# A graph-attention layer with residual and norm: x of row blocks 22 and 23 moved behind the adjacency, added by GpSimd and normalised by VectorE

## The chip, the cores and the metric

The kernel runs on one core of a Trainium2 chip. The metric is the device time of one execution in microseconds. The kernel before takes 233.9 us, the median of 3 runs (233.88 to 234.27).

## The reference

x is 4096 x 512, adj is 4096 x 4096, W is 512 x 2048 (four heads of 512 columns), a holds two vectors of 512 for each head; all are fp32. What is computed:

```python
ht = (x @ W).reshape(N, 4, 512).transpose(1, 0, 2)
e = leaky_relu(src[:, :, None] + dst[:, None, :], 0.01) + adj[None]
att = softmax(e, axis=-1)
out = layernorm(x + einsum('hij,hjd->hid', att, ht).mean(axis=0))
```

`src` and `dst` are the products of `ht` with the halves of `a`. The entries of adj are zero or go up to 1e9, so that in nearly every row the softmax is one at the largest entry of adj and zero elsewhere.

## The kernel before

**What a row needs.** The kernel finds, for each row of adj, the column of its largest entry, gathers that row of x (`y`), multiplies it with the mean of the four heads of W (`w_sum`), adds the row's own x and normalises. A test at the end (`bound`, `test`, `count`, `report`) compares the lead of the largest entry over the second with a bound from the norms of x, W and a; where it fails, a general path (`general`) computes the block in full. With these inputs the general path does not run.

**Blocks.** The 4096 rows are 32 blocks of 128 (`ib` 0 to 31). The names used below: `P` = 128, `NB` = 32, `Q` = 4, `LATE` = 28, `BEHIND` = 24. One block of adj is 2 MB in a tile `adj_t` of a pool with six buffers; one block of x is 256 KB in a row of `hold`, which also holds the results until they are stored.

**The loop.** Step `t` runs over 0 to 31. In step t the sync queue (SP) issues the load of adj block t + 5, ahead of it in some steps a load of x (`x_at`, `load_x`). VectorE takes the segment maxima of adj block t (L212), finds the segment of the largest entry (`find_segment`), and, one or two steps later, the column inside the segment (`find_column`). GpSimd computes the addresses and starts the two gathers for a block: the segment of adj (`lead`, L230) and the row of x (`y`, L250 and L255). TensorE and ScalarE work on block t - 3: `spread` and `from_table` for rows whose partner lies in block 0, `turn` (the transposes at L284 and the copy `yt` at L286), `residual` (x added by a product with the identity, L296) and `products` with `w_sum` (L303). Statistics and normalising (`row_norm`, `parked_stats`, `root`, `scales`, `finish`) follow on ScalarE and GpSimd some steps later.

**The blocks from 24 on.** Blocks 24 to 27 have no residual product. Their sums are copied from PSUM by `put_by` into a spare tile of the adj pool; x of 24 to 27 is loaded into `hold` behind adj 31, and GpSimd adds it in the drain (`add_x`, L357). From block 25 on the last product of a block is put off behind the next block's transposes. Blocks 28 to 31 are normalised by VectorE (`moments`, `factor`, `normalise`).

**The drain.** Behind the loop an order written out by hand follows: the last row norms, the stores of finished blocks, the last two columns (block 31 by an index over the whole row, L278), the last turns and products, the test, and the statistics of 24 to 31 between them. `bound(0)` is a reduction of `xx`, the row norms, on VectorE (`xm`, L498) and a small transpose on TensorE (`px`, L500); `bound(2)` is a product (L505), and `bound(3)` writes `lead_by` on ScalarE (L507). The program order is the order of execution on each engine: nothing is reordered by a scheduler.

Of the kernel before, what the change touches and what calls it, by code (L numbers as in the profile page):

```python
# [9 lines left out]
F32 = mybir.dt.float32  # L10
# [3 lines left out]
AF = mybir.ActivationFunctionType  # L14
# [7 lines left out]
P = 128  # L22
# [51 lines left out]
def leading_rows(ctx, tc, x, adj, W, a, out, ident, leads, any_bad):  # L74
# [8 lines left out]
    nc = tc.nc  # L83
    N, D = x.shape
    H = a.shape[0]
    KB, NB = D // P, N // P
    RB = NB - 1
    AHEAD = 5
    Q = 4
    PIECES = 4  # L90
    LATE = NB - Q
    BEHIND = LATE - Q

    landing = ctx.enter_context(tc.tile_pool(name="landing", bufs=1))
    landing.tile([P, 24], F32, name="pad")
    hold = landing.tile([P, NB, D], F32, name="hold")
    a_rows = landing.tile([2 * H, D], F32, name="a_rows")
    adj_pool = ctx.enter_context(tc.tile_pool(name="adj_pool", bufs=AHEAD + 1))
# [11 lines left out]
    x_rows = x[P:, :].rearrange("(p nb) d -> p nb d", nb=RB)  # L110
# [4 lines left out]
    w_at = NB - KB * H  # L115
    w_sum = once.tile([P, KB, D], F32, name="w_sum")
    adj_t = {}

    def pieces(ib):
        return PIECES if ib == NB - 1 else 2 if ib >= LATE else 1  # L120
# [9 lines left out]
    def load_x(lo, n):  # L130
        if lo == 0:
            nc.sync.dma_start(hold[:, 0, :], x[:P, :])
            lo, n = 1, n - 1
        if n:
            nc.sync.dma_start(hold[:, ds(lo, n), :], x_rows[:, ds(lo - 1, n), :])

    def load_w(kb, n):
        nc.sync.dma_start(hold[:, ds(w_at + kb * H, n * H), :], w_blocks[:, ds(kb * H, n * H), :])
# [17 lines left out]
    for e, lo, hi in spans:  # L156
        if lo == 0:
            nc.gpsimd.iota(first[:, 0:1], pattern=[[0, 1]], base=0, channel_multiplier=N // e)
            lo = 1
# [28 lines left out]
    xx = once.tile([P, NB], F32, name="xx")  # L188
# [9 lines left out]
    seg_of, at_of, lead_of, y_t, yt_of, o_ps = {}, {}, {}, {}, {}, {}  # L198
# [64 lines left out]
    def find_inner(ib):  # L263
        nc.vector.max(out=inner[:, ib, :], in_=lead_of[ib])  # L264

    def find_column(ib):
        if ib < BEHIND:
            find_inner(ib)
# [20 lines left out]
    def turn(ib):  # L289
        yt_of[ib] = turned_rows(y_t.pop(ib))  # L290
# [7 lines left out]
    def products(ib, lo=0, hi=KB):  # L298
        start = ib not in o_ps
        if start:  # L300
            o_ps[ib] = psum.tile([P, D], F32, name="o")
        for kb in range(lo, hi):
            nc.tensor.matmul(  # L303
                o_ps[ib], yt_of[ib][:, kb, :], w_sum[:, kb, :],
                start=(start and kb == 0), stop=(kb == KB - 1),
            )
# [37 lines left out]

    def row_norm(ib):
        sq = rows.tile([P, D], F32, name="sq")
        nc.scalar.activation(sq, hold[:, ib, :], AF.Square, accum_out=xx[:, ib : ib + 1])  # L347

    def put_by(ib):

        if ib == BEHIND:
            o_ps["by"] = adj_pool.tile([P, N // D, D], F32, name="adj_t")
        nc.scalar.copy(o_ps["by"][:, ib - BEHIND, :], o_ps.pop(ib))

    def add_x(ib):
        o = o_ps[ib] = o_ps["by"][:, ib - BEHIND, :]
        nc.gpsimd.tensor_add(o, o, hold[:, ib, :])  # L357

    def add_sums(ib, out):
        nc.vector.tensor_add(out, o_ps[ib], hold[:, ib, :])  # L360
# [2 lines left out]
    def stats(ib):  # L363
        o, i = o_ps[ib], slice(ib, ib + 1)
        sq = rows.tile([P, D], F32, name="sq")
        nc.scalar.activation(sq, o, AF.Identity, scale=-1.0 / D, accum_out=nm[:, i])
        sq = rows.tile([P, D], F32, name="sq")
        nc.scalar.activation(sq, o, AF.Square, bias=nm[:, i], accum_out=sd[:, i])  # L368
# [10 lines left out]
    def scales(i):  # L379
        nc.gpsimd.tensor_mul(nm[:, i], nm[:, i], sd[:, i])  # L380
        nc.gpsimd.tensor_scalar(sd[:, i], sd[:, i], -float(D), None, op0=OP.mult)
# [6 lines left out]
    def finish(ib):  # L388
        i = slice(ib, ib + 1)
        o = hold[:, ib, :] if ib < BEHIND else o_ps.pop(ib)  # L390
        nc.scalar.activation(hold[:, ib, :], o, AF.Identity, bias=nm[:, i], scale=sd[:, i])  # L391
# [15 lines left out]
    def moments(ib):  # L407

        if ib < NB - 1:
            st = small.tile([P, nc.vector.BN_STATS_DIM], F32, name="st", bufs=2)  # L410
            nc.vector.bn_stats(st, o_ps[ib])
        else:
            st = halves_st
        mv = mean_var[ib] = small.tile([P, nc.vector.BN_AGGR_DIM], F32, name="mv", bufs=3)
        nc.vector.bn_aggr(mv, st)
        r = rt[ib] = sd[:, ib : ib + 1]
        nc.scalar.activation(r, mv[:, 1:2], AF.Sqrt, bias=eps)

    def factor(ib, shift=False):
        nc.vector.reciprocal(rt[ib], rt[ib])  # L420
        if shift:
            nc.vector.scalar_tensor_tensor(
                nm[:, ib : ib + 1], mean_var[ib][:, 0:1], -1.0, rt[ib], op0=OP.mult, op1=OP.mult
            )

    def normalise(ib, o, columns=slice(0, D)):
        nc.vector.tensor_scalar(
            hold[:, ib, columns], o, mean_var[ib][:, 0:1], rt[ib], op0=OP.subtract, op1=OP.mult
        )
# [12 lines left out]
    def store(queue, lo, n):  # L442
        if lo == 0:
            queue.dma_start(out[:P, :], hold[:, 0, :])
            lo, n = 1, n - 1
        queue.dma_start(out_rows[:, ds(lo - 1, n), :], hold[:, ds(lo, n), :])
# [82 lines left out]
    def report(pg):  # L529
        nc.vector.tensor_scalar(any_bad, pg, -1.0, float(N), op0=OP.mult, op1=OP.add)  # L530

    x_at = {lo - 1 - lo // (5 * Q): (lo, Q) for lo in range(Q, BEHIND, Q)}
    squares = list(range(KB * H))
    squares_at = {t: 2 if t < 7 else 1 for t in range(3, 15)}
    COLUMN, PROJECT, STATS = 2, 3, 4
    FACTORS = (*((lo, lo + Q) for lo in range(0, BEHIND - Q, Q)), (BEHIND - 4, BEHIND - 2), (BEHIND - 2, BEHIND))
    FINISHED = {t: (t - 11,) for t in range(11, 28)}
    FINISHED |= {28: (17, 18), 29: (19, 20)}

    def lag_of(hi):  # L540
        return hi - 1 + STATS + (3 if hi < BEHIND - 2 else 2)

    WHOLE = range(12, 20)
    END = (*range(1, 3), *range(5, 20))
# [1 line left out]
    for t in range(NB):  # L546
        if t == NB // 2:
            tc.mark_branch_hint_location("general", engines=HINTED)
        if t in x_at:
            load_x(*x_at[t])  # L550
        if t + AHEAD == NB - 1:
            load_x(LATE, 2)
        load_adj(t + AHEAD)
        middle = PIECES if t in END else 1 if t == NB - 1 else 2
        segment_maxima(t, 0, middle)
        if t >= COLUMN and t not in END and t != COLUMN + 1:
            find_column(t - COLUMN)
            if t == lag_of(BEHIND) + 1:
                scales(slice(BEHIND - 2, BEHIND))
        if t not in END:  # L560
            segment_maxima(t, middle, PIECES)
        if t == NB - 1:
            for ib in (BEHIND, LATE + 2, BEHIND + 2):
                load_x(ib, 2)
        find_segment(t)
        if t in END:
            find_column(t - 1 if t <= COLUMN else t - COLUMN)
        if t + 1 in TABLED:
            clear_rows(t + 1)
        for lo, hi in FACTORS:  # L570
            if t == lag_of(hi):
                nc.vector.reciprocal(sd[:, lo:hi], sd[:, lo:hi])
                if hi < BEHIND:
                    scales(slice(lo, hi))
        if t < 2:
            mean_of_heads(t)
        elif t == 2:
            mean_of_heads(2)
            mean_of_heads(3)
            fill_table()  # L580
        if t == 0:
            square_sums_of_a()
        if 21 <= t < 24:
            head_norms(t - 21)
        ib = t - PROJECT
        if t == NB - 2:
            finish(BEHIND - 3)
            finish(BEHIND - 2)
        if t == NB - 1:
            row_norm(LATE)  # L590
            row_norm(LATE + 1)
            finish(BEHIND - 1)
            residual(LATE + 1)
        if ib >= 0:
            if ib in TABLED:
                spread(ib)
            turn(ib)
            if ib > BEHIND:
                products(ib - 1, KB - 1, KB)
            if ib < BEHIND:  # L600
                residual(ib)
            if ib in TABLED:
                from_table(ib)
            products(ib, 0, KB if ib < BEHIND else KB - 1)
            if ib == 0:
                split_table()
        for _ in range(squares_at.get(t, 0)):
            square_sum_of_w(squares.pop(0))
        if t >= BEHIND + STATS:
            put_by(t - STATS)  # L610
        elif t >= STATS:
            row_norm(t - STATS)
            parked_stats(t - STATS)
        for lo, hi in FACTORS:
            if t == hi - 1 + STATS:
                root(slice(lo, hi))
        for done in FINISHED.get(t, ()):
            finish(done)

    for ib in (BEHIND, LATE + 2):  # L620
        row_norm(ib)
        row_norm(ib + 1)
    for ib in range(0, BEHIND - Q, 2):
        store(nc.sync, ib, 2)
    store(nc.sync, BEHIND - Q, Q)
    find_column(NB - 2)
    add_x(BEHIND)
    add_x(BEHIND + 1)
# [4 lines left out]
    turn(NB - 3)  # L633
    row_norm(BEHIND + 2)
    row_norm(BEHIND + 3)
    nc.scalar.activation(xx, xx, AF.Sqrt, scale=1.05 ** 2)
    residual_in_halves(NB - 1)
    products(NB - 3, 0, 2)
    stats(BEHIND)
    bound(0)  # L640
    add_sums(LATE, o_ps[LATE])
# [230 lines left out]
```

## Time and profile before

| what | value |
|---|---|
| median of 3 runs | 233.9 us (233.88 to 234.27) |
| the profiled execution's own time | 233.53 us |
| its span, first to last instruction | 232.0 us |
| bytes moved by DMA | 96.04 MB at a mean of 414 GB/s |
| mean granted TensorE clock | 0.98 |

The page of the profile gives the busy time of each engine as a share of the span, then the span in 40 slices of 5.8 us with the busy share of each slice in tenths. The chain of work that ended last is followed back from the last instruction: at each step to what released it, or to the instruction before it on its engine. A row of the timeline gives start, length, engine, line and operation, the tile written and those read, the shapes and the count; in brackets stand the engine's idle time before it and what ended that. PE is TensorE, DVE VectorE, ACT ScalarE, POOL GpSimd and SP the sync engine. A line such as L357 can be that of a helper, so blocks are told apart by time. A DMA's landing is counted from its issue.

### The profile page before, as it was taken

How to read it: one execution, taken by the hardware profiler on the slowest of the kernel's cores; microseconds unless marked ns; L12 is line 12 of the kernel's file. 1: busy time of each engine (PE TensorE's matmuls, PEld its weight loads, DVE VectorE, ACT ScalarE, POOL GpSimd, SP SyncE). 2: the span in 40 equal slices, each digit the busy share in tenths (PEclk: the TensorE clock that was granted, in tenths of full speed). 3: DMA queues.
4: the chain of work that ended last, by engine and by line, in shares of the span. 5: the costliest groups of instructions: out<-in, count | busy, mean ns of one | idle time of the engine just before them, and what ended most of it. 6: DMA issues, size and time to landing. Idle time of an engine off the chain costs nothing.

```text
span 232.0 us, 2532 instructions
## 1 busy us (share of the span) xinstructions
PE 197.6 (85%) x604; PEld 95.5 (41%) x614; DVE 189.6 (82%) x296; ACT 153.2 (66%) x378; POOL 111.5 (48%) x254
## 2 busy tenths in 40 slices
PE   0069988779099999997999899999999999999990
PEld 0033443334044444443444345454544444545460
DVE  0448289899879997999699959996999999967882
ACT  3003213588075987797998678878888877958872
POOL 4020414525554556355635665554565665637620
PEclk9999999999859999999999999999999999999997
DMA  6999999999999999999999999999999999999995
GB/s 221 426 435 428 433 421 437 425 431 411 440 429 422 420 437 427 429 421 434 418 433 430 417 435 429 419 430 431 426 432 415 419 425 416 419 416 419 420 374 207
DMA packets 13379, 96.04 MB, mean 414 GB/s; under 512 B 2148, under 2 KB 2596, under 8 KB 7984
## 3 DMA queue, kind: packets, MB, share of 16 engines
q1 hardware_dynamic: 9792, 88.08, 90.0%
q0 software_dynamic: 3552, 7.73, 8.5%
q8 instruction: 6, 0.10, 0.2%
q14 instruction: 13, 0.11, 0.1%
q10 hardware_dynamic: 16, 0.02, 0.0%
HBM read 88.51 MB, written 8.39 MB: 418 GB/s over the span
## 4 chain that ended last, share of the span: by engine, by line
DMA 44%; PE 30%; DVE 19%; ACT 2%; issue 1%; POOL 1%; DVEq 0%; POOLq 0%; ACTq 0%
DMA adj_t<-in_adj_dram 39%; PE o L303 19%; DVE seg L212 15%; DMA y<-in_x_dram,col 4%; PE o L296 3%; PE o L343 3%; PE tp L284 3%; PE o L400 2%; DVE at L224 1%; DVE top L222 1%; DMA a_rows<-in_L_gnn_a_dram 1%; DVE inner L264 1%; POOL lead L230 0%; PE o L396 0%; ACT sq L368 0%
## 5 line engine op out<-in xcount | busy, mean ns | idle before, releaser
L212 DVE TENSOR_REDUCE seg<-adj_t 128x128 f32<-128x2048 f32 (+4 forms) x54 | 138.9, 2589 | 27.4 <-DMA adj_t<-in_adj_dram 27.4
L303 PE MATMUL o<-w_sum,yt 128*128 128x512 f32 x248 | 113.5, 598 | 1.1 <-ACT yt L286 0.8
L303 PEld LDWEIGHTS o<-w_sum,yt 128*128 128x128 f32 x248 | 46.8, 192 | 49.0 <-issue 42.0
L230 POOL DMA_INDIRECT lead<-in_adj_dram,row x31 | 32.5, 1050 | 14.5 <-POOL row L226 14.5
L255 POOL DMA_INDIRECT y<-in_x_dram,col x27 | 29.1, 1077 | 12.1 <-POOL col L272 6.1
L226 POOL TENSOR_TENSOR row<-at,first 128x1 uint32<-128x1 uint32 x31 | 5.8, 188 | 60.0 <-DVE at L224 43.6
L284 PE MATMUL tp<-ident,y 128*128 128x128 f32 x128 | 22.9, 302 | 12.0 <-DMA y<-in_x_dram,col 11.9
L286 ACT COPY yt<-tp 128x512 f32<-128x512 f32 x33 | 19.0, 576 | 14.2 <-PE tp L284 13.9
L451 PE MATMUL o<-hold,ident 128*128 128x512 f32 x32 | 16.4, 671 | 14.0 <-DMA hold<-in_L_gnn_W_dram 14.0
L284 PEld LDWEIGHTS tp<-ident,y 128*128 128x128 f32 x128 | 18.3, 210 | 23.9 <-issue 17.8
L296 PE MATMUL o<-hold,ident 128*128 128x512 f32 x50 | 26.5, 612 | 0.0
L333 ACT ACTIVATE off<-px,minus 128x128 f32<-128x128 f32 x27 | 9.9, 366 | 19.9 <-PE px L331 19.8
L343 PE MATMUL o<-z,pick 128*128 128x512 bf16 x72 | 20.4, 386 | 1.1 <-ACT pick L335 0.8
L347 ACT ACTIVATE sq<-hold 128x512 f32<-128x512 f32 x32 | 20.0, 625 | 0.0
L391 ACT ACTIVATE hold<-hold,nm,sd 128x512 f32<-128x512 f32 x24 | 18.8, 801 | 0.0
L374 ACT ACTIVATE sq<-hold,nm 128x512 f32<-128x512 f32 x24 | 17.3, 722 | 0.8
L452 ACT ACTIVATE w_sum<-o 128x512 f32<-128x512 f32 x4 | 2.4, 597 | 22.5 <-PE o L451 22.5
L245 ACT COPY y<-zero 128x512 f32<-128x512 f32 x27 | 16.3, 603 | 0.0
L451 PEld LDWEIGHTS o<-hold,ident 128*128 128x128 f32 x32 | 6.7, 216 | 22.9 <-issue 21.6
L343 PEld LDWEIGHTS <-pick 128*128 128x128 bf16 x81 | 7.8, 100 | 19.9 <-issue 10.5
L372 ACT ACTIVATE hold<-o 128x512 f32<-128x512 f32 x24 | 14.3, 597 | 0.8
L222 DVE MAX8 top<-seg 128x8 f32<-128x256 f32 (+2 forms) x31 | 11.3, 366 | 1.1
(117 smaller groups left out, 190.3 us busy)
## 6 DMA issues: line engine op xcount, KB each, us to landing
adj_t<-in_adj_dram SPq DMA_DIRECT2D x28, 2048.0 KB, 33.1
adj_t<-in_adj_dram SPq DMA_DIRECT2D x6, 1024.0 KB, 27.3
out_dram<-hold SPq DMA_DIRECT2D x12, 512.0 KB, 10.1
hold<-in_x_dram SPq DMA_DIRECT2D x5, 1024.0 KB, 33.0
hold<-in_L_gnn_W_dram SPq DMA_DIRECT2D x2, 2048.0 KB, 16.5
hold<-in_x_dram SPq DMA_DIRECT2D x4, 512.0 KB, 12.7
adj_t<-in_adj_dram SPq DMA_DIRECT2D x4, 512.0 KB, 18.6
out_dram<-hold SPq DMA_DIRECT2D x4, 256.0 KB, 2.8
```

What stands on the lines that cost most here:

```text
L212: nc.vector.tensor_reduce(seg_of[ib][:, ts(k, N // e // n)], adj_t[ib][:, ts(k, N // n)].rearrange("p (s e) -> p s e", e=e), axis=AX.X, op ...
L230: nc.gpsimd.indirect_dma_start(out=lead, out_offset=None, in_=adj_segs[e], in_offset=bass.IndirectOffsetOnAxis(ap=row[:, :1], axis=0),)
L255: nc.gpsimd.indirect_dma_start(out=y_t[ib], out_offset=None, in_=x, in_offset=bass.IndirectOffsetOnAxis(ap=col[:, :1], axis=0), bounds_che ...
L284: nc.tensor.transpose(tp[:, kb, :], y[:, ds(kb, P, KB)], ident)
L286: nc.scalar.copy(yt, tp)
L296: nc.tensor.matmul(o_ps[ib], ident, hold[:, ib, :], start=start, stop=False)
L303: nc.tensor.matmul(o_ps[ib], yt_of[ib][:, kb, :], w_sum[:, kb, :], start=(start and kb == 0), stop=(kb == KB - 1),)
L343: nc.tensor.matmul(o_ps[ib], pick, z[k], start=(start and k == 0), stop=False)
L347: nc.scalar.activation(sq, hold[:, ib, :], AF.Square, accum_out=xx[:, ib : ib + 1])
L374: nc.scalar.activation(sq, hold[:, ib, :], AF.Square, bias=nm[:, i], scale=-float(D), accum_out=sd[:, i])
L391: nc.scalar.activation(hold[:, ib, :], o, AF.Identity, bias=nm[:, i], scale=sd[:, i])
L451: nc.tensor.matmul(o, ident, hold[:, w_at + kb * H + h, :], start=(h == 0), stop=(h == H - 1))
```

## The change

`PUT` = 22 is new. Blocks 22 and 23 join the path of blocks 24 to 27, with these differences: x of 22 to 27 is loaded behind adj 31 into a spare tile of the adj pool (`late_x`), the sums of 22 to 27 are copied from PSUM into `hold`, and GpSimd adds there in place. Blocks 22 and 23 lose their residual product, their parked statistics on ScalarE, their root, factors and finish; instead VectorE takes their moments and normalises them in the drain, ahead of `bound(0)`. x of 20 and 21 is loaded alone in step 19, where x of 20 to 23 was loaded in step 18. The row norms of 28 and 29 move from step 31 to step 30. The row norms of 22 and 23 move into the drain, ahead of those of 24, 25, 30 and 31. The stores of blocks 0 to 7 go out in fours, and the store of 20 to 23 is split in two.

```diff
+    PUT = BEHIND - 2
...
+    late_x = []
...
-            nc.sync.dma_start(hold[:, ds(lo, n), :], x_rows[:, ds(lo - 1, n), :])
+            to = late_x[0][:, ds(lo - PUT, n), :] if PUT <= lo < LATE else hold[:, ds(lo, n), :]
+            nc.sync.dma_start(to, x_rows[:, ds(lo - 1, n), :])
...
     def row_norm(ib):
         sq = rows.tile([P, D], F32, name="sq")
-        nc.scalar.activation(sq, hold[:, ib, :], AF.Square, accum_out=xx[:, ib : ib + 1])
+        x_of = late_x[0][:, ib - PUT, :] if PUT <= ib < LATE else hold[:, ib, :]
+        nc.scalar.activation(sq, x_of, AF.Square, accum_out=xx[:, ib : ib + 1])
 
     def put_by(ib):
-
-        if ib == BEHIND:
-            o_ps["by"] = adj_pool.tile([P, N // D, D], F32, name="adj_t")
-        nc.scalar.copy(o_ps["by"][:, ib - BEHIND, :], o_ps.pop(ib))
+        nc.scalar.copy(hold[:, ib, :], o_ps[ib])
+        o_ps[ib] = hold[:, ib, :]
 
     def add_x(ib):
-        o = o_ps[ib] = o_ps["by"][:, ib - BEHIND, :]
-        nc.gpsimd.tensor_add(o, o, hold[:, ib, :])
+        nc.gpsimd.tensor_add(o_ps[ib], o_ps[ib], late_x[0][:, ib - PUT, :])
...
-    x_at = {lo - 1 - lo // (5 * Q): (lo, Q) for lo in range(Q, BEHIND, Q)}
+    x_at = {lo - 1: (lo, Q) for lo in range(Q, BEHIND - Q, Q)}
+    x_at[PUT - 3] = (BEHIND - Q, 2)
...
-    FACTORS = (*((lo, lo + Q) for lo in range(0, BEHIND - Q, Q)), (BEHIND - 4, BEHIND - 2), (BEHIND - 2, BEHIND))
+    FACTORS = (*((lo, lo + Q) for lo in range(0, BEHIND - Q, Q)), (BEHIND - Q, PUT))
...
-            if t == lag_of(BEHIND) + 1:
-                scales(slice(BEHIND - 2, BEHIND))
...
         if t == NB - 1:
-            for ib in (BEHIND, LATE + 2, BEHIND + 2):
+            late_x.append(adj_pool.tile([P, N // D, D], F32, name="adj_t"))
+            for ib in (PUT, BEHIND, LATE + 2, BEHIND + 2):
                 load_x(ib, 2)
...
         if t == NB - 2:
             finish(BEHIND - 3)
-            finish(BEHIND - 2)
-        if t == NB - 1:
             row_norm(LATE)
             row_norm(LATE + 1)
-            finish(BEHIND - 1)
+        if t == NB - 1:
             residual(LATE + 1)
...
-            if ib < BEHIND:
+            if ib < PUT:
                 residual(ib)
...
-        if t >= BEHIND + STATS:
+        if t >= PUT + STATS:
             put_by(t - STATS)
...
-    for ib in (BEHIND, LATE + 2):
+    for ib in (PUT, BEHIND, LATE + 2):
         row_norm(ib)
         row_norm(ib + 1)
-    for ib in range(0, BEHIND - Q, 2):
+    for ib in range(0, 2 * Q, Q):
+        store(nc.sync, ib, Q)
+    for ib in range(2 * Q, PUT, 2):
         store(nc.sync, ib, 2)
-    store(nc.sync, BEHIND - Q, Q)
+    add_x(PUT)
+    add_x(PUT + 1)
     find_column(NB - 2)
     add_x(BEHIND)
     add_x(BEHIND + 1)
...
     row_norm(BEHIND + 2)
     row_norm(BEHIND + 3)
+    moments(PUT)
+    moments(PUT + 1)
     nc.scalar.activation(xx, xx, AF.Sqrt, scale=1.05 ** 2)
     residual_in_halves(NB - 1)
     products(NB - 3, 0, 2)
+    for ib in (PUT, PUT + 1):
+        factor(ib)
+        normalise(ib, o_ps.pop(ib))
+    store(nc.sync, PUT, 2)
     stats(BEHIND)
     bound(0)
     add_sums(LATE, o_ps[LATE])
```

More of the change, by code (lines that the diff above doesn't have):

```diff
@@ L540, in lag_of @@
     def lag_of(hi):
-        return hi - 1 + STATS + (3 if hi < BEHIND - 2 else 2)
+        return hi - 1 + STATS + (3 if hi < PUT else 2)
     WHOLE = range(12, 20)
@@ L572, in leading_rows @@
                 nc.vector.reciprocal(sd[:, lo:hi], sd[:, lo:hi])
-                if hi < BEHIND:
-                    scales(slice(lo, hi))
+                scales(slice(lo, hi))
         if t < 2:
```

## The prediction

> **What bounds the kernel now.** I read the page's engine and DMA rows first, then the chain of work that ended last, then the timelines of the four engines from block 22 on.
>
> ```profile
> PE 197.6 (85%) x604; PEld 95.5 (41%) x614; DVE 189.6 (82%) x296; ACT 153.2 (66%) x378; POOL 111.5 (48%) x254
> DMA  6999999999999999999999999999999999999995
> DMA packets 13379, 96.04 MB, mean 414 GB/s; under 512 B 2148, under 2 KB 2596, under 8 KB 7984
> ```
>
> Three resources are near full at once. The DMA engines are full in every slice but the first and the last, and the change moves no byte more or less: it can only reorder them. So the question is which work waits for which in the last 30 us.
>
> ```profile
> 215.42 0.11 PE px L500
> 215.53 0.86 PE o L303 x2
> 216.39 0.32 PE px L505 x2
> ...
> 216.74 0.35 ACT lead_by L507
> ...
> 221.68 0.70 ACT hold L391
> 222.38 0.48 ACT yt L286
> ```
>
> The chain passes through one narrow place in the drain: the small transpose px at L500 (`bound(0)`), which needs VectorE's `xm`, then px at L505, then ScalarE's `lead_by`. Behind it the chain follows ScalarE's square roots and statistics to `yt` of block 31 and its products, with hand-overs of some hundredths: whatever delays px at L500 delays the end.
>
> **The change part by part.**
>
> *The x loads.* Before, 1 MB of x (blocks 20 to 23) stands in the queue ahead of adj 23. Now half of it stands ahead of adj 24, and x of 22 and 23 follows adj 31.
>
> ```profile
> 158.53 2.29 DVE L212 TENSOR_REDUCE seg<-adj_t 128x64 f32<-128x2048 f32 x1 [2.00 <-DMA adj_t<-in_adj_dram]
> 164.16 2.28 DVE L212 TENSOR_REDUCE seg<-adj_t 128x64 f32<-128x2048 f32 x1
> L128 SPq DMA_DIRECT2D adj_t<-in_adj_dram x1: 327/327/327, 130.2 to 130.2; - x1
> DMA to landing us min/median/max: 33.8/33.8/33.8
> ...
> 208.46 0.09 DVE L270 MATCH_VALUE_LOAD within<-top,lead 128x8 f32 x1 [1.83 <-DMA lead<-in_adj_dram,row]
> 208.77 4.42 DVE L278 FIND_INDEX8 col<-top,adj_t 128x8 uint32<-128x4096 f32 x1
> 214.91 0.18 DVE L498 TENSOR_REDUCE xm<-xx 128x1 f32<-128x32 f32 x1 [1.72 <-ACT xx L636]
> ```
>
> The first row is block 23: VectorE waited 2.00 us for it. With 1 MB (1.05 MB / 414 GB/s = 2.5 us) gone from in front, that wait goes. What is late next is adj 24: issued at 130.2, it landed 33.8 us later, at 164.0, and VectorE started on it at 164.16. It has 0.52 MB less in front, 1.27 us. From 164.16 to the wait at 208.46 VectorE's timeline shows no gap of its own, so all of it moves by 1.27 us: the index of block 31 (208.77 + 4.42 = 213.19) ends at 211.92. The gathers of y move along. The load of x for 20 and 21 comes one step later and is not needed until four steps after that: nothing. On SP the extra load of x takes the place of one store, and its queue stays full before and after: nothing.
>
> *TensorE.* Blocks 22 and 23 lose their residual matmuls.
>
> ```profile
> 177.14 0.70 PE L284 MATMUL tp<-ident,y 128*128 128x128 f32 x4
> 182.67 0.70 PE L284 MATMUL tp<-ident,y 128*128 128x128 f32 x4
> 188.21 0.70 PE L284 MATMUL tp<-ident,y 128*128 128x128 f32 x4
> 189.40 0.59 PE L343 MATMUL o<-z,pick 128*128 128x512 bf16 x2 [0.49 <-ACT pick L335]
> 192.46 0.70 PE L284 MATMUL tp<-ident,y 128*128 128x128 f32 x4
> ```
>
> A block with a residual takes 182.67 - 177.14 = 5.53 us. The residual was also the cover for ScalarE's pick. Block 24 has none: 192.46 - 188.21 = 4.25 us, plus two products put off into the next block (0.86, by the chain's row at 215.53) = 5.11 us, with an idle gap before the pick in it. So each block gains 0.42 us and not the whole residual, 0.84 together. One tenth is lost again where two row norms move to step 30 of ScalarE, ahead of the pick of block 27 (an estimate: its timeline shows no idle time there). TensorE enters the drain about 0.75 us early; the gathers, 1.27 early, keep ahead of it.
>
> *ScalarE.*
>
> ```profile
> 208.81 0.59 ACT L353 COPY adj_t<-o 128x512 f32<-128x512 f32 x1 [0.27 <-PE o L303]
> 209.30 0.63 ACT L347 ACTIVATE sq<-hold 128x512 f32<-128x512 f32 x1
> 209.92 0.62 ACT L347 ACTIVATE sq<-hold 128x512 f32<-128x512 f32 x1
> 212.80 0.59 ACT L286 COPY yt<-tp 128x512 f32<-128x512 f32 x1 [0.94 <-PE tp L284]
> 213.28 0.63 ACT L347 ACTIVATE sq<-hold 128x512 f32<-128x512 f32 x1
> 214.65 0.23 ACT L636 ACTIVATE xx<-xx 128x32 f32<-128x32 f32 x1
> 216.99 0.28 ACT L417 ACTIVATE sd<-mv,eps 128x1 f32<-128x1 f32 x1
> ```
>
> In the loop it loses two parked statistics, one root and the finishes of 22 and 23, and gains two copies: it is off the path there, so nothing. In the drain it gains the row norms of 22 and 23 and two square roots. The copy at 208.81 follows TensorE and moves to 208.06, so the norms start at 208.55 instead of 209.30. Six of them at a pitch of 0.62 end at 212.25 (the 0.94 us of idle time before the `yt` copy is used up), the `yt` copy takes 0.48 to the next start, and two more norms end at 213.97. The square root of 22 follows to 214.26, that of 23 to 214.45, and `xx` is done at 214.6, a quarter of a microsecond earlier than now.
>
> *VectorE in the drain.*
>
> ```profile
> 215.81 0.68 DVE L411 BATCH_NORM_STATS2 st<-o 128x6 f32<-128x512 f32 x1
> 216.52 0.18 DVE L415 BATCH_NORM_AGGREGATE mv<-st 128x2 f32<-128x6 f32 x1
> 217.30 0.16 DVE L420 RECIPROCAL sd<-sd 128x1 f32<-128x1 f32 x1 [0.60 <-ACT sd L417]
> 217.50 0.81 DVE L427 TENSOR_SCALAR hold<-o,mv,sd 128x512 f32<-128x512 f32 x1
> ...
> 225.56 0.55 DVE L427 TENSOR_SCALAR hold<-hold,mv,sd 128x512 f32<-128x512 f32 x1
> 227.98 0.54 DVE L427 TENSOR_SCALAR hold<-o,mv,sd 128x256 f32<-128x256 f32 x1
> ```
>
> Two moments, 2 x (0.68 + 0.18) = 1.72 us, run from 211.92 to 213.65. They lie in the 1.72 us for which VectorE stood idle before `xm`: nothing. The two reciprocals and normalisations have no such cover. They need ScalarE's root (214.26) and stand ahead of `xm` in VectorE's order. From SBUF, as here, a normalisation takes 0.55; with the reciprocal, the hand-over and the overlap with the next, about 0.67 each. `xm` so starts at 215.6 and ends at 215.8, against 214.91 and 215.09 now.
>
> ```profile
> 213.47 1.96 PE L303 MATMUL o<-w_sum,yt 128*128 128x512 f32 x4
> 215.26 0.27 PE L500 MATMUL px<-ident,xm 128*1 128x128 f32 x1
> ...
> 208.84 0.19 POOL L272 TENSOR_TENSOR col<-start,within 128x1 uint32<-128x1 uint32 x1 [3.73 <-PE o L303]
> 213.95 0.97 POOL L250 DMA_INDIRECT y<-in_x_dram,col  x1 [0.88 <-PE o L396]
> 214.94 2.51 POOL L357 TENSOR_TENSOR adj_t<-adj_t,hold 128x512 f32<-128x512 f32 x2
> ```
>
> TensorE executes in order. It comes to px at about 214.6 and stands there until 215.82: **0.56 us later than the 215.26 of now**. The 0.75 us won in the loop are spent waiting, and what is queued behind px (the rest of block 29, the turn of block 30, and `lead_by` on ScalarE) starts 0.56 late.
>
> *GpSimd.* The two adds of 22 and 23 (2.51 us a pair) fall into its 3.73 us of idle time before 208.84: x of 22 and 23 follows adj directly, so nothing. They also stand ahead of `col` of block 30, so a landing of x later than about 205 would cost what it is late. The gather of block 31 moves from 213.95 to 212.7, and the adds of 26 and 27 from 214.94 to 213.7, ending at 216.2. The normalisations want to run at 214.5 and 215.1, **in the middle of these adds**. What that costs no row shows, so it is bounded. Lower end: 0, as for VectorE's index at 208.77, beside which a pair of GpSimd adds runs at the usual length; a gain is excluded, since nothing is taken away. Upper end: they exclude each other for a whole instruction. Then the first normalisation waits for the add that ends at 214.94 and ends at 215.5; the second add runs to 216.8; the second normalisation ends at 217.35 and px starts at 217.47, 2.2 us later than now. (With both adds first it comes out the same within 0.1.) I take the upper end. From PSUM 256 columns take 0.54 and 512 take 0.81, so a column costs 1.05 ns and the fixed part is 0.27; from SBUF 512 columns take 0.55, so a column costs half of that. That row is of an operation that fetches two columns at a time, and it ran when GpSimd had no add left. The rows without a clash are of operations at one column a time (4.42 us / 4096 = 1.08 ns), so they stand further off.
>
> The Trainium skill ("SBUF — State Buffer", "Who interferes with whom") says that a VectorE `tensor_scalar` in its two-port mode and a GpSimd instruction hold a shared port pair exclusively, each for its whole length, while a one-input VectorE operation outside that mode does not contend. The index beside the adds agrees with the second half; no run so far shows the first. By it the sum would be +2.2 us, without it +0.6 us.
>
> *The sum.* Loop -0.75 (spent at the wait), moments 0, normalisations +0.56 at px, clash +1.65: +2.2 us at px. Behind it all hangs on ScalarE and VectorE in order. Is there slack? Only TensorE has some:
>
> ```profile
> 221.28 0.72 PE L284 MATMUL tp<-ident,y 128*128 128x128 f32 x4 [0.26 <-DMA y<-in_x_dram,col]
> ```
>
> The last gather was 0.26 us late for TensorE and now comes earlier. But `yt` of block 31 waits for ScalarE's `hold` (chain, 221.68 to 222.38), and that runs through `lead_by`. So the 2.2 us reach the end. The profiled execution took 233.53 us for a span of 232.0; the median of the runs is 233.9. 233.9 + 2.2 = **236.1 us**.
>
> **The rivals.**
>
> *No clash.* The normalisations run beside the adds at 0.55. For: the unhurt index. Against: it is another kind of operation. 233.9 + 0.56 = 234.5 us.
>
> *One wait only.* Both normalisations get in between the two adds: `xm` is 0.5 late instead of 1.65. 233.9 + 0.56 + 0.5 = 234.95 us. Against: the second add is ready at once.
>
> *Faster: the wait at px does not bind.* If `xm` is ready by the time TensorE gets there (about 214.6), the 0.75 us pass on to px, `lead_by` and the end: 233.15 us. It decides at one point, `xm` ending before 214.6 rather than 215.8. For: adj really lands earlier. Against: even with ScalarE's roots at once, VectorE has 1.72 + 1.35 us of new work after 211.92, so `xm` cannot end before 215.1, as now.
>
> **How the numbers follow.** A clash with +2.2: 50%; one wait: 15%; no clash: 22%; faster: 8%; the rest (the loop's shifts smaller, or a late x ahead of `col`) 5%. The likeliest has its own range of 235.7 to 236.5. The range of 8 in 10 goes down to 234.2, which leaves out the faster case and a quarter of the no-clash case, and up to 236.6. Under 0.2% (0.47 us) this kernel's runs cannot tell from no change. Faster by more than that 0.08; within it 0.12 (a third of the no-clash case and part of the rest); slower 0.80.
>
> **What would show it.** VectorE's 2.00 us wait for adj 23 gone and its blocks from 24 on some 1.27 us earlier; 5.1 us for blocks 22 and 23 on TensorE; moments of 22 right after the index, at about 212; an idle TensorE before px at L500, ended by `xm`; the normalisations of 22 and 23 late against the roots, with the first starting where an add of GpSimd ends. Wrong it would be if px at L500 came before 215, if the normalisations ran at once beside the adds, or if the part behind `lead_by` shrank.

## The result and the profile after

The changed kernel takes **235.09 us** (median of 5 runs, 234.94 to 235.45), the kernel before 233.9 us beside it (5 runs, 233.88 to 234.28). The ratio is 1.0048, 95% interval [1.0035, 1.0061]: slower by 1.2 us, where 2.2 us were forecast. The profiled execution took 235.17 us for a span of 233.5 us, against 233.53 and 232.0.

The page's engine and DMA rows:

```profile
PE 197.3 (84%) x610; PEld 94.8 (41%) x610; DVE 193.2 (83%) x303; ACT 149.4 (64%) x371; POOL 113.4 (49%) x254
DMA  6999999999999999999999999999999999999974
DMA packets 13379, 96.04 MB, mean 411 GB/s; under 512 B 2148, under 2 KB 2596, under 8 KB 8112
```

The bytes are the same. VectorE has 3.6 us more work, ScalarE 3.8 us less, and the last two slices of the DMA row are emptier. The totals don't say why the end is later; the places named in the prediction do. The line numbers are now up by one to three (px is L501). First VectorE's timeline:

```profile
156.87 2.27 DVE L215 TENSOR_REDUCE seg<-adj_t 128x64 f32<-128x2048 f32 x1
162.72 2.29 DVE L215 TENSOR_REDUCE seg<-adj_t 128x64 f32<-128x2048 f32 x1 [0.15 <-DMA adj_t<-in_adj_dram]
...
206.72 0.09 DVE L273 MATCH_VALUE_LOAD within<-top,lead 128x8 f32 x1 [1.53 <-DMA lead<-in_adj_dram,row]
207.03 4.42 DVE L281 FIND_INDEX8 col<-top,adj_t 128x8 uint32<-128x4096 f32 x1
211.37 0.68 DVE L412 BATCH_NORM_STATS2 st<-hold 128x6 f32<-128x512 f32 x1
...
214.53 0.16 DVE L421 RECIPROCAL sd<-sd 128x1 f32<-128x1 f32 x1 [1.48 <-ACT sd L418]
214.73 1.26 DVE L428 TENSOR_SCALAR hold<-hold,mv,sd 128x512 f32<-128x512 f32 x1
216.10 0.55 DVE L428 TENSOR_SCALAR hold<-hold,mv,sd 128x512 f32<-128x512 f32 x1
216.56 0.18 DVE L499 TENSOR_REDUCE xm<-xx 128x1 f32<-128x32 f32 x1
```

The first row is block 23, without the wait of 2.00 us that it had before. The second is block 24, which starts 1.44 us earlier (164.16 before). The last index ends at 211.45, 1.74 us earlier. The moments run in the idle time behind it. Then the two normalisations stand ahead of `xm`, and **the first takes 1.26 us, the second 0.55**: same operation, same shape. The reason stands in GpSimd's timeline:

```profile
208.92 2.52 POOL L358 TENSOR_TENSOR hold<-hold,adj_t 128x512 f32<-128x512 f32 x2
212.21 0.97 POOL L253 DMA_INDIRECT y<-in_x_dram,col  x1 [0.78 <-PE o L306]
213.20 2.50 POOL L358 TENSOR_TENSOR hold<-hold,adj_t 128x512 f32<-128x512 f32 x2
```

The adds of 26 and 27 end at 215.70; the normalisation that began at 214.73 ends at 215.99, 0.29 us behind them. TensorE and ScalarE:

```profile
177.39 0.70 PE L287 MATMUL tp<-ident,y 128*128 128x128 f32 x4
182.51 0.70 PE L287 MATMUL tp<-ident,y 128*128 128x128 f32 x4
187.62 0.70 PE L287 MATMUL tp<-ident,y 128*128 128x128 f32 x4
...
213.13 1.98 PE L306 MATMUL o<-w_sum,yt 128*128 128x512 f32 x4
216.80 0.27 PE L501 MATMUL px<-ident,xm 128*1 128x128 f32 x1 [1.68 <-DVE xm L499]
```

```profile
208.34 0.59 ACT L354 COPY hold<-o 128x512 f32<-128x512 f32 x1 [0.28 <-PE o L306]
214.22 0.47 ACT L418 ACTIVATE sd<-mv,eps 128x1 f32<-128x1 f32 x2
229.63 0.56 ACT L441 ACTIVATE hold<-o,nm,sd 128x256 f32<-128x256 f32 x1 [0.43 <-DVE nm L423]
```

Blocks 22 and 23 take 5.12 and 5.11 us on TensorE. It is early in the drain and then stands 1.68 us before px, which runs at 216.80 instead of 215.26: **1.54 us late**. The last half block on ScalarE (229.63) starts 12.83 us behind px, as before the change (228.09 - 215.26): the way from px to there kept its length. The chain of waits shows the new way to px:

```profile
214.31 0.20 ACT sd L418
214.53 0.17 DVE sd L421
214.73 1.26 DVE hold L428
...
216.56 0.19 DVE xm L499
216.80 0.27 PE px L501
```

A held-up operation looks like a long operation here: the chain puts 1.26 us on VectorE and doesn't name GpSimd.

### The profile page after: what moved, and what is told of

It is laid out like the page before. It is cut to its first block, busy times and chain, and to the rows that moved or that the text cites. A ratio compares the mean times of both kernels' runs of the same rounds, so it can differ in the third digit from the quotient of the medians.

```text
span 233.5 us, 2534 instructions
## 1 busy us (share of the span) xinstructions
PE 197.3 (84%) x610; PEld 94.8 (41%) x610; DVE 193.2 (83%) x303; ACT 149.4 (64%) x371; POOL 113.4 (49%) x254
## 4 chain that ended last, share of the span: by engine, by line
DMA 54%; DVE 24%; PE 14%; ACT 5%; issue 1%; DVEq 0%; ACTq 0%
DMA adj_t<-in_adj_dram 53%; DVE seg L215 19%; PE o L306 9%; ACT sq L351 2%; PE o L346 2%; PE o L401 2%; DVE at L227 1%; DVE top L225 1%; DMA a_rows<-in_L_gnn_a_dram 1%; DVE hold L428 1%; PE tp L287 1%; DVE within L273 1%; DVE inner L267 1%; ACT sd L418 0%; ACT yt L289 0%
## 5 line engine op out<-in xcount | busy, mean ns | idle before, releaser
L452 PE MATMUL o<-hold,ident 128*128 128x512 f32 x32 | 16.5, 677 | 14.0 <-DMA hold<-in_L_gnn_W_dram 14.0
L299 PE MATMUL o<-hold,ident 128*128 128x512 f32 x46 | 24.4, 614 | 0.0
L346 PE MATMUL o<-z,pick 128*128 128x512 bf16 x81 | 22.6, 389 | 1.0 <-ACT pick L338 0.8
L392 ACT ACTIVATE hold<-hold,nm,sd 128x512 f32<-128x512 f32 x26 | 20.5, 802 | 0.0
L375 ACT ACTIVATE sq<-hold,nm 128x512 f32<-128x512 f32 x22 | 15.9, 722 | 0.7
L351 ACT ACTIVATE sq<-hold 128x512 f32<-128x512 f32 x26 | 16.2, 624 | 0.0
L373 ACT ACTIVATE hold<-o 128x512 f32<-128x512 f32 x22 | 13.1, 597 | 0.7
```

Source lines behind the costliest of these rows:

```text
L299: nc.tensor.matmul(o_ps[ib], ident, hold[:, ib, :], start=start, stop=False)
L346: nc.tensor.matmul(o_ps[ib], pick, z[k], start=(start and k == 0), stop=False)
L351: nc.scalar.activation(sq, x_of, AF.Square, accum_out=xx[:, ib : ib + 1])
L452: nc.tensor.matmul(o, ident, hold[:, w_at + kb * H + h, :], start=(h == 0), stop=(h == H - 1))
```

## The experiments

Theory: two causes at one place. The reciprocals and normalisations stand ahead of `xm` in VectorE's order (about 0.8 us at px), and GpSimd's adds hold the first of them up (0.7 us). Rivals: the 1.26 us have another reason; the loss is in the loop or in the stores. Each kernel was timed beside the kernel before, which stood at 234.0 to 234.1 us in every comparison; diffs are against the changed kernel if nothing else is said, and the name in brackets is the one used for the kernel further down.

**Without the adds of 26 and 27 (no_adds_26).** This kernel leaves x out of these two blocks.

```diff
-    add_x(BEHIND + 2)
-    add_x(BEHIND + 3)
```

> The changed kernel without the two GpSimd adds of blocks 26 and 27 (x is not added to these two blocks; everything else as before). In the changed kernel the normalisation of block 22 took 1.26 us instead of 0.55 and ended 0.29 us after GpSimd's pair of adds, and px at L501 came at 216.80. Theory (the two exclude each other): without the adds the normalisation of 22 takes 0.55, px comes 0.7 us earlier, at about 216.1, and the time falls by 0.7 us from 235.1 to about 234.4. Rival (the normalisation is slow for itself, or waits for something else, such as a late root or a full queue): still 1.26 us, px at 216.8, time 235.1.

Measured: 234.58 us, ratio 1.0022 [1.0011, 1.0033]. VectorE and TensorE:

```profile
215.04 0.55 DVE L428 TENSOR_SCALAR hold<-hold,mv,sd 128x512 f32<-128x512 f32 x1
216.39 0.27 PE L501 MATMUL px<-ident,xm 128*1 128x128 f32 x1 [0.96 <-DVE xm L499]
```

The operation is back at 0.55 us. So the 0.71 us are the adds'. px came only 0.41 us earlier, because ScalarE's roots were 0.31 us later in this execution (214.53 against 214.22). Taking the adds away gives back 0.5 us of the 1.2; the rest of the loss is still there without them.

**Two more adds behind them (two_more_adds).** The outputs of these two are not used, so nothing can wait for their data.

```diff
+    for k in (6, 7):
+        nc.gpsimd.tensor_add(late_x[0][:, k, :], late_x[0][:, 0, :], late_x[0][:, 1, :])
```

> The changed kernel with two more GpSimd adds of the same size (into unused columns of the spare tile) behind those of 26 and 27; they need nothing else and nothing needs them. Theory A (a waiting VectorE operation gets in when the running add ends): the normalisation of 22 ends near 216.0 as now, the one of 23 waits for the third add, to about 217.5; px 1.0 to 1.4 us later than 216.80, time about 236.3. Theory B (GpSimd keeps the path through its adds as long as they follow each other at once): the normalisation of 22 ends near 218.3, px at about 219.1, time about 237.4. Rival (no exclusion): px at 216.8 and 235.1 as now.

Measured: 238.72 us, ratio 1.0206 [1.0166, 1.0246]. VectorE, GpSimd and TensorE:

```profile
214.60 3.39 DVE L428 TENSOR_SCALAR hold<-hold,mv,sd 128x512 f32<-128x512 f32 x1
```

```profile
212.78 2.49 POOL L358 TENSOR_TENSOR hold<-hold,adj_t 128x512 f32<-128x512 f32 x2
215.22 2.48 POOL L634 TENSOR_TENSOR adj_t<-adj_t 128x512 f32<-128x512 f32 x2
```

```profile
218.80 0.37 PE L501 MATMUL px<-ident,xm 128*1 128x128 f32 x1 [3.81 <-DVE xm L499]
218.97 1.91 PE L306 MATMUL o<-w_sum,yt 128*128 128x512 f32 x2
```

Four adds end at 217.70, the normalisation at 217.99. The normalisation came in the second add (half of the first pair's 2.49 us was over at 214.03) and did not get in at either of the two seams behind it (a seam is where one add ends and the next begins): adds that follow each other act as one, as Theory B had it. The rows leave no gap at the seam between the pairs (212.78 + 2.49 = 215.27, and the next pair starts at 215.22). The Trainium skill ("SBUF — State Buffer", "Who interferes with whom") says that VectorE in a two-port mode and GpSimd exclude each other for a whole instruction, and that whoever issues first has it; the traces agree that VectorE's wait is whole, and show it lasting over three instructions in a row. That GpSimd waits for VectorE as well, no run shows, and in the last experiment the operation that starts first in the trace is the one that waits.

px is 2.0 us later than in the changed kernel, but the time 3.6 us. The rest arose behind px: the last half block on ScalarE starts 14.82 us behind it (233.62 - 218.80), not 12.83. There the granted clock of TensorE is halved. It is the third column from the right in the table by stretches of time (behind it the DMA share and GB/s); here for this kernel:

```profile
218.80:220.00 1.20, 1.20 (x3) 0.51 (x3) 1.20 (x3) 0.00 (x0) 0.00 (x0) 0.50 1.02 416
220.00:222.00 2.00, 2.00 (x7) 1.18 (x6) 0.32 (x3) 0.53 (x2) 0.00 (x0) 0.50 1.02 416
222.00:224.00 2.00, 2.00 (x6) 0.94 (x5) 1.72 (x9) 1.49 (x4) 0.00 (x0) 0.50 0.55 225
```

and of the changed kernel:

```profile
216.80:218.80 2.00, 2.00 (x10) 1.23 (x11) 1.51 (x4) 0.53 (x2) 0.00 (x0) 1.00 1.03 420
```

Behind TensorE's wait of 3.81 us the clock is 0.50 for the 5.2 us of these rows, and two products take 1.91 us (1.02 in the changed kernel); behind the wait of 1.68 us it stays at 1.00. The Trainium skill ("TensorE: Matmul & The Clock Gate", "Part 1: The HAM clock gate") gives half rate after an idle window of about 3.4 us. The two waits lie on either side of that, but the fall came sooner: at about 217.7, some 2.7 us behind the last product (213.00 + 1.98 = 214.98). At the ends of the executions, where TensorE has nothing left to do, the clock falls between 2.2 us (no_adds_26: 227.76 to about 229.9) and 5.2 us (changed kernel: 228.16 to about 233.4) behind the last product. So the shortest idle time ahead of a fall was about 2.2 us here.

**The row norms of 22 and 23 earlier, in step 31 (early_norms).**

```diff
         if t == NB - 1:
+            row_norm(PUT)
+            row_norm(PUT + 1)
...
-    for ib in (PUT, BEHIND, LATE + 2):
+    for ib in (BEHIND, LATE + 2):
```

> The changed kernel with the row norms of 22 and 23 moved from the drain into the end of step 31, ahead of the turn of block 28, where ScalarE stands idle for 3.85 us and x of 22 and 23 has landed (by 205). ScalarE's chain to the roots gets 1.2 us shorter, so the roots of 22 and 23 come at about 213.4. Theory with exclusion: the normalisation of 22 then meets the first add of 26 and 27 (213.2 to 214.5); if it gets in between the adds, that of 23 waits for the second, px at about 216.5, time 234.8; if GpSimd keeps the path through both, px at 216.8 as now, 235.1. Rival (no exclusion, ScalarE's longer chain is the cause): px 1.2 us earlier, at 215.6, time 233.9.

Measured: 234.99 us, ratio 1.0056 [1.0031, 1.0080]. The premise missed: ScalarE's roots came no earlier, because the `yt` copy ahead of them waits for TensorE.

```profile
212.43 0.59 ACT L289 COPY yt<-tp 128x512 f32<-128x512 f32 x1 [0.94 <-PE tp L287]
214.15 0.47 ACT L418 ACTIVATE sd<-mv,eps 128x1 f32<-128x1 f32 x2
```

```profile
214.66 0.68 DVE L428 TENSOR_SCALAR hold<-hold,mv,sd 128x512 f32<-128x512 f32 x1
```

```profile
212.54 2.50 POOL L358 TENSOR_TENSOR hold<-hold,adj_t 128x512 f32<-128x512 f32 x2
```

As a test of the roots it is inconclusive. It gives another size of the hold-up: here the adds ended at 215.04 and the normalisation at 215.34, 0.30 behind, so it took 0.68 us only. A second run of the unaltered changed kernel (median 235.11 us, ratio 1.0066 [1.0044, 1.0087]) has 0.88 us in its profile:

> The changed kernel once more, unaltered, timed beside the three above. Both theories: 1.1 to 1.3 us over the kernel before.

```profile
214.64 0.88 DVE L428 TENSOR_SCALAR hold<-hold,mv,sd 128x512 f32<-128x512 f32 x1
216.33 0.27 PE L501 MATMUL px<-ident,xm 128*1 128x128 f32 x1 [1.30 <-DVE xm L499]
```

Its adds ended at 215.23. In each of the four executions so far in which the adds held the first normalisation up, px started 1.10 us behind the end of GpSimd's adds (215.70 to 216.80, 217.70 to 218.80, 215.04 to 216.14, 215.23 to 216.33). So with the hold-up GpSimd's adds set px; without it, as in no_adds_26, ScalarE's root does.

**The normalisations moved behind the bound (late_norm).** The other cause alone: 22 and 23 are normalised behind `moments(LATE - 1)`, and their store goes out with the last ones. Their moments have to be kept for longer, so `mv` gets five buffers in place of three.

```diff
-        mv = mean_var[ib] = small.tile([P, nc.vector.BN_AGGR_DIM], F32, name="mv", bufs=3)
+        mv = mean_var[ib] = small.tile([P, nc.vector.BN_AGGR_DIM], F32, name="mv", bufs=5)
...
-    for ib in (PUT, PUT + 1):
-        factor(ib)
-        normalise(ib, o_ps.pop(ib))
-    store(nc.sync, PUT, 2)
     stats(BEHIND)
...
     moments(LATE - 1)
+    for ib in (PUT, PUT + 1):
+        factor(ib)
+        normalise(ib, o_ps.pop(ib))
...
-    for ib, n in ((LATE, 2), (BEHIND, 2), (BEHIND + 2, 2), (NB - 2, 1)):
+    for ib, n in ((LATE, 2), (PUT, 2), (BEHIND, 2), (BEHIND + 2, 2), (NB - 2, 1)):
```

> The changed kernel with the two reciprocals and normalisations of 22 and 23 (and their store) moved behind the moments of block 27, where VectorE waits 0.71 us for a root. Theory (they stand ahead of xm in VectorE's order, and that alone makes the change slower): xm follows the root of xx at 214.8, px comes at about 215.05 instead of 216.80, TensorE no longer waits there for 1.68 us, and the time falls by 1.5 to 1.7 us to 233.4 to 233.6, at or just under the kernel before. Rival (only the clash with GpSimd costs anything): 234.4. Rival (the later x or the stores in another order make it slower): 235.1, with px early and the end unmoved.

Measured: 234.21 us, ratio 1.0007 [0.9997, 1.0016].

```profile
214.80 0.19 DVE L499 TENSOR_REDUCE xm<-xx 128x1 f32<-128x32 f32 x1 [1.99 <-ACT xx L639]
215.04 0.27 PE L501 MATMUL px<-ident,xm 128*1 128x128 f32 x1
```

px comes at 215.04 with no wait on TensorE, 0.22 us before the kernel before: part of the loop's gain has reached it. So the whole loss at px lies in these four instructions and their place. The time misses the expected 233.4 to 233.6 us. ScalarE's last half block starts 0.22 us earlier than in the kernel before (227.87 against 228.09), but the DMA engines end later. The likely reason is the 0.5 MB of store that has moved into the last microseconds; no run tests that by itself. The stretch from 230 to 232 us of this kernel, then of the kernel before (second column from the right, the DMA share: 0.27 against 0.14):

```profile
230.00:232.00 2.00, 0.00 (x0) 0.00 (x0) 0.00 (x0) 0.00 (x0) 0.00 (x0) 0.51 0.27 101
```

```profile
230.00:232.00 2.00, 0.00 (x0) 0.00 (x0) 0.00 (x0) 0.00 (x0) 0.00 (x0) 0.50 0.14 51
```

**The normalisations in VectorE's idle time, and GpSimd behind them (own_slot).** Row norms early as above; moments, roots and normalisations right behind the last index; and a tiny GpSimd copy that reads the normalised block 23, so that the adds of 26 and 27 wait for it.

```diff
     find_column_in_row(NB - 1)
+    moments(PUT)
+    moments(PUT + 1)
+    for ib in (PUT, PUT + 1):
+        factor(ib)
+        normalise(ib, o_ps.pop(ib))
+    store(nc.sync, PUT, 2)
+    behind_norm = once.tile([P, 1], F32, name="behind_norm")
+    nc.gpsimd.tensor_copy(behind_norm, hold[:, PUT + 1, 0:1])
     add_x(BEHIND + 2)
...
-    moments(PUT)
-    moments(PUT + 1)
...
-    for ib in (PUT, PUT + 1):
-        factor(ib)
-        normalise(ib, o_ps.pop(ib))
-    store(nc.sync, PUT, 2)
```

> The changed kernel with three moves: the row norms of 22 and 23 at the end of step 31; the moments, reciprocals and normalisations of 22 and 23 (and their store) straight behind the index of block 31, with their roots ahead of ScalarE's yt copy of block 29; and the GpSimd adds of 26 and 27 behind a one-column GpSimd copy that reads block 23's result, so that they cannot start before the normalisations end. Theory (place ahead of xm, clash, and in the late variant the late store): the normalisations take 0.55 each and end near 213.8, the adds follow until 216.3, xm follows ScalarE at about 214.5, TensorE comes to px at 215.0 without waiting, and the last store is issued 0.2 to 0.3 us earlier than in the kernel before and lands 2.35 us later again: 0.2 to 0.3 us under the kernel before, 233.7. Rival (moving 22 and 23 costs something by itself: the later x, the stores, the work in all): 234.5 or more. Rival (the adds of 26 and 27, now 1.2 us later, are late for the statistics of 26): the end 0.5 us later.

Measured: 234.02 us, ratio 1.0000 [0.9991, 1.0008]. Both normalisations take 0.55 us and the loss is gone, but there is no gain:

```profile
213.82 1.98 PE L306 MATMUL o<-w_sum,yt 128*128 128x512 f32 x4 [0.72 <-ACT yt L289]
215.64 0.27 PE L501 MATMUL px<-ident,xm 128*1 128x128 f32 x1
```

The roots now stand ahead of the `yt` copy of block 29 on ScalarE; TensorE waits 0.72 us for that, and px is 0.38 us later than before the change. A new wait has taken the place of the old one.

Two side questions went with it: whether the turn of block 31 set ahead of `finish(BEHIND)` in the drain's order lets TensorE's last products start sooner, in own_slot (own_slot_turn) and in the kernel before (before_turn).

```diff
-    finish(BEHIND)
     turn(NB - 1)
+    finish(BEHIND)
```

> The one above, and on ScalarE the yt copy of block 31 ahead of the finish of block 24. In the kernels before, yt waits 0.3 us for that finish and TensorE stands 0.35 us. Theory (the end hangs on yt of block 31): the last products and the end 0.35 us earlier than in the one above, 233.3. Rival (the stores bound the end by now): no gain over the one above.

> The kernel before, with the yt copy of block 31 ahead of the finish of block 24 and nothing else, so that this part can be told from the rest. There TensorE got its gather of block 31 0.26 us late, and yt came 0.29 us after the transposes. Theory: 0.25 to 0.3 us faster, 233.65. Rival (the gather of 31 bounds it, or the stores): no gain.

Measured: 234.28 us, ratio 1.0007 [0.9999, 1.0016], and 234.30 us, ratio 1.0011 [0.9997, 1.0025]. Neither gains. In own_slot_turn TensorE's last products start 0.32 us earlier than in own_slot (222.96 against 223.28), but ScalarE finishes blocks 26 and 27 0.36 us later (from 225.96, not 225.60), and the DMA share from 230.5 to 231.0 us is 0.83 instead of 0.26. In before_turn TensorE won nothing in the profiled execution: its gather of block 31 was 0.46 us late, not 0.26, the last products started at 222.91 as before, and blocks 26 and 27 were finished 0.68 us later. That the later stores cost what was won fits this, but was not tested by itself.

**As own_slot, the `yt` copy between the two roots (own_slot_yt).** Against own_slot:

```diff
     moments(PUT)
-    moments(PUT + 1)
+    products(LATE, KB - 1, KB)
+    turn(NB - 3)
+    moments(PUT + 1)
...
-    products(LATE, KB - 1, KB)
-    turn(NB - 3)
```

> As own_slot, but ScalarE copies yt of block 29 between the two square roots and not behind both. Theory (what own_slot lost at px, 0.38 us, is the yt copy that stood behind the roots, so that TensorE's products of block 29 started 0.72 us late): the copy runs at about 212.5, products at 213.1, xx is done at about 214.8, xm at 215.0 finds VectorE free, px at 215.1 to 215.2, that is 0.1 us before the kernel before; normalisations still 0.55 us each, GpSimd's adds behind them at about 214.4. The time is then 233.7 to 233.9. Rival (the last stores bound the end, whatever px does): px as said, last half finished 0.1 to 0.5 us earlier than in own_slot, but the time 234.0 to 234.2. Third: px at 215.6 or later, another wait in its place, and 234.0 or more.

Measured: **233.52 us**, ratio 0.9977 [0.9968, 0.9986]; run again 233.64 us, ratio 0.9979 [0.9970, 0.9988]. This version beats both kernels, by 0.2% the one before. Its ScalarE, VectorE, GpSimd and TensorE:

```profile
212.28 0.29 ACT L418 ACTIVATE sd<-mv,eps 128x1 f32<-128x1 f32 x1 [0.98 <-DVE mv L416]
212.48 0.56 ACT L289 COPY yt<-tp 128x512 f32<-128x512 f32 x1
```

```profile
213.78 0.55 DVE L428 TENSOR_SCALAR hold<-hold,mv,sd 128x512 f32<-128x512 f32 x1
```

```profile
214.39 0.19 POOL L642 COPY behind_norm<-hold 128x1 f32<-128x1 f32 x1 [1.22 <-DVE hold L428]
```

```profile
215.13 0.27 PE L501 MATMUL px<-ident,xm 128*1 128x128 f32 x1
```

px is 0.51 us earlier than in own_slot and 0.13 earlier than before the change; in the profile of the second run it stood at 215.27. So px can account for the 0.4 to 0.5 us against own_slot, but not for the 0.4 to 0.6 us of the medians against the kernel before. That kernel's traced execution, at 233.53 us, is faster than its median, and a comparison of single traces can't show where this gain lies. It stays open. What was expected of the second run:

> The kernel own_slot_yt unaltered, on the same chip as no_guard: 233.5 us, 0.5 us under the kernel before if its gain is real; 233.9 or more if it was a matter of that batch.

**The same without the small GpSimd copy (no_guard).** Against own_slot_yt:

```diff
-    behind_norm = once.tile([P, 1], F32, name="behind_norm")
-    nc.gpsimd.tensor_copy(behind_norm, hold[:, PUT + 1, 0:1])
```

> As own_slot_yt, without the small GpSimd copy that reads the normalised block 23: the adds of 26 and 27 no longer wait for VectorE and start behind the gather, at about 213.2. The normalisation of 22 starts at 213.12, that of 23 wants to start at 213.78. Theory (an operation that has begun holds the other up, and GpSimd's adds that follow each other let nothing in between): the normalisation of 22 takes 0.55, the first add waits for it until about 213.7; that of 23 then meets the pair of adds (213.7 to 216.2) and ends about 0.3 us behind it, at 216.5, as one operation of some 2.7 us; px at 216.9, 1.8 us later than in own_slot_yt, and 235.2 us. Rival (the copy is worth little, since the normalisation of 23 gets in between the two adds): it ends by 215.3, px at 215.6, 0.5 us later, and 234.0. Second rival (with the place and not the order of GpSimd as the cause, no clash at all): px at 215.1 and 233.5.

Measured: 235.08 us, ratio 1.0041 [1.0026, 1.0055].

```profile
213.34 2.86 DVE L428 TENSOR_SCALAR hold<-hold,mv,sd 128x512 f32<-128x512 f32 x1
216.31 0.55 DVE L428 TENSOR_SCALAR hold<-hold,mv,sd 128x512 f32<-128x512 f32 x1
```

```profile
213.41 2.50 POOL L358 TENSOR_TENSOR hold<-hold,adj_t 128x512 f32<-128x512 f32 x2
```

```profile
217.00 0.27 PE L501 MATMUL px<-ident,xm 128*1 128x128 f32 x1 [1.70 <-DVE xm L499]
```

px moved by 1.73 us against the second run of own_slot_yt (1.87 against the first), and the time by 1.4: one copy of 0.19 us, whose result nobody needs, is worth that much, because it puts GpSimd behind VectorE. The price is as the theory had it. The order within it is not: the normalisation of 22 was the one held up. It stands in the trace 0.07 us ahead of the adds, and they went first all the same. Nor did it get in at the seam between the two adds. px again starts 1.09 us behind their end (215.91).

## Why the prediction was right, and where it was off

*The loop: right.* The 2.00 us wait for block 23 went, VectorE came 1.44 us early (1.27 forecast), and TensorE's blocks 22 and 23 took 5.12 and 5.11 us (5.11 forecast). TensorE entered the drain 0.47 us early by ScalarE's copy (208.34 against 208.81), not 0.75; a gather of y for block 17 had set it back to 0.25 us behind the kernel before (149.16 against 148.91). As forecast, what it won was spent standing before px; late_norm shows that 0.22 us of it would have counted there.

*Moments free, normalisations on the path: right.* The moments lay in VectorE's idle time. The reciprocals and normalisations ahead of `xm` were put at +0.56; without the hold-up the trace gives 1.54 - 0.71 = +0.83. The missing 0.27 is TensorE's smaller lead, which brought the copy 0.28 and the roots 0.25 us later than worked out.

***The clash: right in kind, mis-sized.*** This is the term that failed: +1.65 was taken and 0.71 measured. The prediction let the first normalisation in between the two adds, and the second wait for the second add. The trace shows one wait, for the rest of the second add, and none for the second normalisation; the first did not start where an add ends, which the prediction had named as a sign, but inside the second add. The step behind it is the time of the adds: they were put at 213.7 to 216.2 and ran at 213.20 to 215.70, because the last index ended at 211.45 and not at 211.92 (the `lead` ahead of it came 1.74 us earlier, not 1.27). The first add was over when the normalisation came. By the 1.10 us above the end of the pair sets px, so 0.5 us of the 0.67 between the forecast 217.47 and the measured 216.80 are this shift. The other 0.17 is the seam that the forecast counted on: 1.10 behind an end at 216.2, px would have been at 217.3. The prediction did note the order with both adds first, and put it within 0.1 of the other.

*The sum.* +2.2 was forecast at px, +1.54 measured; the normalisations cost 0.27 more than forecast and the clash 0.94 less. The two profiled executions differ by 1.64 us, the medians by 1.2, since the profiled one of the kernel before was faster than its median. The part behind `lead_by` kept its length, as forecast. The measured 235.09 us lies below the likeliest case's own range (235.7 to 236.5); that the whole range holds it is luck in part, since its lower end was there for cases with no clash or a smaller one.

*The rivals.* "No clash" (234.5) is out by no_adds_26: the adds hold VectorE up. "One wait only" (234.95) comes close in time, but its mechanism, both normalisations in the seam between the adds, is not what happened: here the normalisation met the second add alone, and where it met a seam, in two_more_adds and no_guard, it did not get in. "Faster" (233.15) named the right point, `xm` ending before TensorE gets to px; none of the orders tried here reached its time, and the best came to 233.52.

## What to carry to other kernels

Work moved to an engine that has idle time is free only where it stands in that engine's order: here the moments cost nothing, and two normalisations a few lines below cost 0.8 us, since a small reduction that TensorE waits for was queued behind them. Before a VectorE operation like this normalisation (`tensor_scalar`, SBUF to SBUF) is put beside GpSimd's elementwise work, look at when that work ends, and set one behind the other by a dependency if need be. An operation with two durations at one shape (0.55 and 1.26 us) can be a hidden wait, and the engine that ends just ahead of it is the one to ask.

## What the runs showed of the hardware

VectorE's normalisation (SBUF to SBUF, 128x512) does not get done while GpSimd's adds run. The time is counted into the operation, 0.68, 0.88, 1.26, 2.86 and 3.39 us in place of 0.55, and in all five it ends 0.29 to 0.30 us behind the last add of an unbroken row, whether of two or of four. Some other VectorE operations were not held: in the changed kernel the index over 4096 columns took its 4.42 us beside the adds of 24 and 25 (208.92 to 211.44), and in own_slot_yt `xm` (0.19 us) and statistics read from PSUM (0.68 us) ran at their usual length inside the adds of 26 and 27 (214.54 to 217.03).

The prediction did not expect that the seams between GpSimd's instructions give VectorE no way in (three seams in two kernels), nor did any expectation have adds that start 0.07 us later in the trace go first; why they did, no run shows. An estimate fits both the 0.07 and the 0.29 us: the prediction's split of a normalisation, worked out from its rows of 0.54, 0.81 and 0.55 us, into a fixed 0.27 us and 0.28 for the columns, if only the columns wait. In no_guard they would then have come up at 213.34 + 0.27 = 213.61, behind the start of the adds at 213.41. No run tests this.

And a TensorE wait of 3.81 us cost a second time, as a clock of 0.50 until about 5.6 us behind px (218.80 to about 224.4), where waits of 1.68 and 1.70 us cost nothing of the kind.
